# Layer 1's self-attention on quarters of TensorE's rows: the score products of four heads in two parts and a shift, with the maxima between them

## The chip, the cores and the metric

The kernel runs on one core of a Trainium2 chip. The metric is the device time in microseconds of one execution. Five engines work side by side and wait for each other through semaphores: TensorE (PE, with its weight loads listed as PEld), VectorE (DVE), ScalarE (ACT), GpSimd (POOL) and SyncE (SP), whose queue issues most of the transfers. Three runs of the kernel before took 2361.84, 2367.62 and 2370.89 us; the median is 2367.62.

## What is computed

The reference is a decoder of two layers on x (2 x 1024 tokens of 256). Each layer has self-attention, cross-attention and a feed-forward part, with a layer norm behind each. The change lies in the second layer's self-attention (layer 1), 16 heads of 16 dimensions:

```python
def _L1_attn_ref(x, W_qkv, b_qkv, W_proj, b_proj):
    NUM_HEADS, HEAD_DIM = 16, 16
    qkv = x @ W_qkv + b_qkv
    ...
    scores = jnp.einsum('bhqd,bhkd->bhqk', q, k) * HEAD_DIM ** -0.5
    attn = jax.nn.softmax(scores, axis=-1)
    out = jnp.einsum('bhqk,bhkd->bhqd', attn, v)
    ...
    return out @ W_proj + b_proj
```

The scores are 2 x 16 x 1024 x 1024, and the softmax runs over 1024 keys.

## The kernel before, in words

TensorE multiplies `lhsT` (the weights, loaded first) with `rhs` (streamed, up to 512 columns) into a bank of PSUM. The stacks here are in the format F32R. To keep precision, queries and keys are split by `l1_project` (L1167) into a high part and a rest: `qh`, `ql`, `kh`, `kl`. A product is then (qh + ql)(kh + kl), four partial products of 16 rows each.

`l1_attn` (L1197) handles four heads, a *quad*, at a time. The 16 **steps** (L1259) are batch x quad x half of the queries (512). A step has 8 **units**, one for each 128 keys (`kt`); there are 128 units. `stacks` (L1246) copies the parts by DMA into stacks for two heads each: 64 rows for a head, with the queries as qh, ql, qh, ql and the keys as kh, kh, kl, kl. A matmul of 64 rows so adds all four partial products at once, and two heads of a stack sit on the two halves of TensorE's rows. Each quad has two key and two query stacks: 4 x 8 = 32 transfers of 64 KB. SP's queue issues them, and ScalarE's half of those of the first quad (L1251).

The softmax needs the row maxima before the exponentials. `maxima` (L1262) computes scores with queries as rows: two matmuls (L1277) into two banks of the pool `bank` (three banks, L43 and L58), and VectorE takes the negated maximum of each bank (L1287). A step needs 16 such calls, two to a unit, nine units ahead of the products. `shifts` and `shifted` (L1291, L1303) turn a step's maxima into rows (four small VectorE operations, four transposes on TensorE at L1308, a copy at L70).

`products` (L1314) computes scores with keys as rows, two `wide` tiles (two banks each, two tiles in the pool) to a unit: for each, two matmuls of 64 rows (L1322) and two more (L1328) that add the shift through `pick`, a tile of ones and zeros. ScalarE takes the exponential of each wide tile (L1334). `mix` (L1341) multiplies the weights of the unit before with the values: four heads on four column tiles of 32 (L1348), an ordinary F32 matmul. After each step `taken` and `quotient` (L1355, L1359) copy the sum, transpose it (L1368) and divide.

The order is written out by hand (L1458 to L1488): nine early units of maxima into wide tiles (L1282), with projections and values between them; then for each unit, first call of maxima, products, second call of maxima, at a step's end the shift, then the mix of the unit before, then what `extra` holds for this unit (projections, stacks, values, normalisation). All three of TensorE, VectorE and ScalarE run in exactly this order. The stage begins at about 1690 us and its last mix is near 2160 us.

Of the kernel before, what the change touches and what calls it, by code (L numbers as in the profile page):

```python
# [33 lines left out]
class Decoder:  # L34
# [1162 lines left out]
    def l1_attn(self):  # L1197
        nc, t = self.nc, self.t
        w, parts = self.l1w, self.l1parts
        wo = self.weight(t["L1_attn_W_proj"].rearrange("(c p) o -> p c o", p=P), 2, D)  # L1200
        with ExitStack() as s:
            pool = lambda n, k: s.enter_context(self.pool(n, k))
            one, stp, qkp, rawp = pool("la1", 1), pool("st", 2), pool("qk", 1), pool("raw", 1)
            self.l1qkp = qkp

            pick = []
            for k in range(2):
                f = self.weight(None, 1, P)[:, 0, :]
                nc.gpsimd.memset(f, 0.0)
                for a in range(k, 4, 2):  # L1210
                    nc.gpsimd.memset(f[32 * a : 32 * a + 32, :], 1.0)
                pick.append(one.tile([P, P], F32R, name=f"pick{k}"))
                nc.vector.tensor_copy(pick[k], f)

            zeros = [one.tile([P, 4, 4, 32], F32, name=f"cz{k}") for k in range(2)]
            for cz in zeros:
# [2 lines left out]
            def project(b, m, name, blk):  # L1219
                self.l1_project(b, m, name, blk, self.xT[2 * b + blk])  # L1220
# [21 lines left out]
                    )  # L1242

            stack = {}

            def stacks(b, jp, name):  # L1246

                st = stack[b, jp, name] = stp.tile([P, S], F32R, tag=name, name=f"{name}st", bufs=4)
                for a in range(2):
                    at = 32 * (jp % 4) + 16 * a  # L1250
                    by = nc.scalar if a and b == 0 and jp < 2 else nc.sync  # L1251
                    for i, x in enumerate((0, 1, 0, 1) if name == "q" else (0, 0, 1, 1)):
                        by.dma_start(
                            st[64 * a + 16 * i : 64 * a + 16 * i + 16, :].bitcast(F32),
                            parts[name, b, jp // 4][x][at : at + 16, :],
                        )


            steps = [(b, quad, qb) for b in range(B) for quad in range(4) for qb in range(2)]  # L1259
            most, shift = {}, {}  # L1260

            def maxima(u, early=False):  # L1262

                if u >= 16 * len(steps):
                    return
                n, k = u // 16, u % 16 // 8
                qt, kb = divmod(u % 8, 2)
                b, quad, qb = steps[n]
                jp = 2 * quad + k
                if u % 16 == 0:  # L1270
# [4 lines left out]
                for a in range(2):  # L1275
                    rows = slice(64 * a, 64 * a + 64)
                    nc.tensor.matmul(  # L1277
                        sc[a], lhsT=stack[b, jp, "q"][rows, q0 : q0 + P],
                        rhs=stack[b, jp, "k"][rows, kb * 512 : (kb + 1) * 512], start=True, stop=True,
                    )  # L1280
                if early:
                    nc.vector.tensor_reduce(  # L1282
                        most[n][:, kb, qt, k : k + 3 : 2], both, AX.X, ALU.max, negate=True
                    )
                for a in range(0 if early else 2):
                    h = 2 * a + k
                    nc.vector.tensor_reduce(  # L1287
                        most[n][:, kb, qt, h : h + 1], sc[a], AX.X, ALU.max, negate=True
                    )

            def shifts(n):  # L1291

# [21 lines left out]
            def products(n, kt):  # L1314

                b, quad, qb = steps[n]
                ps = [self.wide(), self.wide()]
                for k in range(2):
                    q, keys = (stack[b, 2 * quad + k, name] for name in "qk")
                    for a in range(2):  # L1320
                        rows = slice(64 * a, 64 * a + 64)
                        nc.tensor.matmul(  # L1322
                            ps[k][:, a, :], lhsT=keys[rows, kt * P : (kt + 1) * P],
                            rhs=q[rows, qb * 512 : (qb + 1) * 512], start=True, stop=False,
                        )
                    for a in range(2):
                        rows = slice(64 * a, 64 * a + 64)
                        nc.tensor.matmul(  # L1328
                            ps[k][:, a, :], lhsT=pick[k][rows, :], rhs=shift[n][rows, :],
                            start=False, stop=True,  # L1330
                        )
                slot = self.weight(None, 2, S)
                for k in range(2):
                    nc.scalar.activation(  # L1334
                        slot[:, k, :], ps[k].rearrange("p a q -> p (a q)"), AF.Exp, scale=0.25
                    )
                return n, kt, slot.rearrange("p k (a q) -> p (k a) q", a=2)

            mixed = {}
# [86 lines left out]
            def at(unit, f, *args):  # L1426
                extra.setdefault(unit, []).append((f, args))
# [4 lines left out]
            last = 8 * len(steps)  # L1432
            both = [(name, blk) for name in "qk" for blk in range(2)]
            for n, (b, quad, qb) in enumerate(steps):
                first = 8 * n
                if qb == 0:
                    for i, (name, blk) in enumerate(both):
                        if quad % 2 == 0 and n > 4:
                            at(first - 26 + i, project, b, quad // 2, name, blk)
                    for i, name in enumerate("qk" if n else ()):  # L1440
                        for k in range(2):
                            at(first - 20 + 2 * k + i, stacks, b, 2 * quad + k, name)
                    if quad == 0 and n:
                        for k in range(4):
                            at(first - 22 + k, values, b, k)
                at(first + 8, taken, n)
                at(first + 9, quotient, n)
                if quad == 3 and n < len(steps) - 1:
                    g = 2 * b + qb
                    for k, f in ((10, turned), (11, output), (13, normed), (15, onward)):  # L1450
                        at(first + k, f, g)

            def others(unit):
                for f, args in extra.pop(unit, ()):
                    f(*args)

            engines = {mybir.EngineType.PE, mybir.EngineType.DVE, mybir.EngineType.Activation}
            with self.tc.manual_schedule(engines=engines):  # L1458
                for k in range(2):
                    for name in "kq":  # L1460
                        stacks(0, k, name)
                jobs = [lambda k=k: values(0, k) for k in range(4)]
                jobs += [lambda a=a: project(0, 1, *a) for a in both]
                for unit in range(-9, 0):
                    maxima(2 * unit + 18, True)
                    maxima(2 * unit + 19, True)
                    if jobs:
                        jobs.pop(0)()
                    others(unit)
                shifts(0)  # L1470
                shifted(0)
                late = None
                for unit in range(last + 1):

                    n = (unit + 1) // 8 if unit % 8 == 7 else None
                    if n:
                        shifts(n)
                    maxima(2 * unit + 18)
                    now = products(*divmod(unit, 8)) if unit < last else None
                    maxima(2 * unit + 19)  # L1480
                    if n:
                        shifted(n)
                    if late:
                        mix(*late)
                    late = now
                    others(unit)
                for unit in sorted(extra):
                    others(unit)  # L1488
# [607 lines left out]
```

## Time and profile before

| | |
|---|---|
| median of three runs | 2367.62 us |
| the profiled execution | 2366.31 us |
| its span, first to last instruction | 2364.4 us |
| mean granted TensorE clock | 0.982 |
| maxima on banks, VectorE (L1287) | 476 of 683 ns |
| matmuls for them (L1277) | 476 of 479 ns |
| products (L1322), shifts (L1328) | 512 each, median 393 ns for L1322 |
| exponentials, ScalarE (L1334) | 256 of 1022 ns |
| mix (L1348) | 1024 of 621 ns in the records |

The profile counts a matmul's time up to its result; the next one starts well before that, so distances between starts are read instead of durations. "Idle before, releaser" at the end of a group's line is the time that the engine stood before these instructions and what ended it. In the timeline, equal instructions that follow each other are merged (x2, x4), with the time of the first start and the time to the last end.

### The profile page before, as it was taken

How to read it: one execution, taken by the hardware profiler on the slowest of the kernel's cores; microseconds unless marked ns; L12 is line 12 of the kernel's file. 1: busy time of each engine (PE TensorE's matmuls, PEld its weight loads, DVE VectorE, ACT ScalarE, POOL GpSimd, SP SyncE). 2: the span in 40 equal slices, each digit the busy share in tenths (PEclk: the TensorE clock that was granted, in tenths of full speed). 3: DMA queues.
4: the chain of work that ended last, by engine and by line, in shares of the span. 5: the costliest groups of instructions: out<-in, count | busy, mean ns of one | idle time of the engine just before them, and what ended most of it. 6: DMA issues, size and time to landing. Idle time of an engine off the chain costs nothing.

```text
span 2364.4 us, 37096 instructions
## 1 busy us (share of the span) xinstructions
PE 2269.4 (96%) x13969; PEld 1568.0 (66%) x13969; DVE 1668.2 (71%) x2902; ACT 1107.6 (47%) x1730; POOL 907.5 (38%) x743
## 2 busy tenths in 40 slices
PE   8999999999998899999999999999999999999985
PEld 4555555555545678999999999999644444554752
DVE  5898888988786346545555555456789687995778
ACT  4666566566553323233233233333156455665346
POOL 4676576676565344413333333333200001002420
PEclk9999999999999999999999999999989999999988
DMA  6777677677685110101010001000303122210001
GB/s 153 175 180 171 150 181 170 146 179 174 140 200 126 41 61 1 36 10 35 19 31 26 29 31 36 15 1 1 70 12 50 19 37 36 41 32 1 1 1 36
DMA packets 103831, 168.67 MB, mean 71 GB/s; under 512 B 47603, under 2 KB 65509, under 8 KB 103653
## 3 DMA queue, kind: packets, MB, share of 16 engines
q1 hardware_dynamic: 96804, 147.94, 27.6%
q10 hardware_dynamic: 6848, 18.36, 3.1%
q8 instruction: 111, 1.82, 0.3%
q14 instruction: 68, 0.55, 0.1%
HBM read 34.10 MB, written 2.10 MB: 15 GB/s over the span
## 4 chain that ended last, share of the span: by engine, by line
PE 83%; DVE 9%; ACT 2%; issue 2%; SPq 2%; DMA 1%; POOL 1%; ACTq 0%; DVEq 0%; POOLq 0%
PE unit L1017 16%; PE acc L1065 10%; PE wide L325 9%; PE acc L410 8%; PE bank L1065 7%; PE acc L1348 5%; PE bank L280 4%; PE bank L1277 3%; DVE most L1287 3%; PE bank L428 2%; PE bank L740 2%; PE bank L304 2%; PE wide L1322 2%; PE wide L1328 2%; SPq L389 1%
## 5 line engine op out<-in xcount | busy, mean ns | idle before, releaser
L340 DVE TENSOR_REDUCE nm<-wide 128x1 f32<-128x1024 f32 x256 | 301.0, 1216 | 67.1 <-PE wide L325 66.0
L1334 ACT ACTIVATE w<-wide 128x1024 f32<-128x1024 f32 x256 | 248.2, 1022 | 142.9 <-PE wide L1328 133.5
L1287 DVE TENSOR_REDUCE most<-bank 128x1 f32<-128x512 f32 x476 | 295.7, 683 | 22.2 <-PE bank L1277 22.1
L325 PE MATMUL wide<-k,q 64*128 64x512 f32 x1024 | 262.4, 625 | 7.5 <-ACT p L345 6.7
L356 POOL TENSOR_SCALAR p<-p,sums 128x1024 f32<-128x1024 f32 x128 | 143.5, 1121 | 255.3 <-DVE sums L353 255.3
L410 PE MATMUL acc<-turned,v 128*64 128x256 f32 x2048 | 236.8, 384 | 3.3 <-DMA wq<-in_L_attn_w_q 3.3
L410 PEld LDWEIGHTS acc<-turned,v 128*64 128x64 f32 x2048 | 142.9, 137 | 115.7 <-issue 43.1
L1006 ACT ACTIVATE mhT<-mhT,cols 128x256 f32<-128x256 f32 (+1 forms) x256 | 143.4, 607 | 146.5 <-DVE mhT L1034 103.4
L345 ACT ACTIVATE p<-wide,nm 128x1024 f32<-128x1024 f32 x128 | 142.7, 1115 | 124.6 <-DVE nm L340 104.6
L915 POOL TENSOR_TENSOR hs<-hs,mhT 128x1024 f32<-128x1024 f32 x31 | 102.4, 3305 | 237.4 <-DVE hs L913 220.2
L1017 PE MATMUL unit<-xT,w 128*128 128x256 f32 x768 | 182.0, 379 | 0.0
L1074 DVE SCALAR_TENSOR_TENSOR r<-acc,gates,r 128x128 f32<-128x128 f32 x256 | 77.8, 345 | 138.1 <-PE acc L1065 138.1
L370 DVE STREAM_TRANSPOSE blocks<-p 128x1024 f32<-128x1024 f32 x128 | 158.1, 1235 | 20.5 <-DMA turned<-blocks 6.1
L325 PEld LDWEIGHTS wide<-k,q 64*128 64x128 f32 x1024 | 90.0, 188 | 121.4 <-issue 87.0
L370 DVE STREAM_TRANSPOSE blocks<-r 128x1024 f32<-128x1024 f32 x128 | 153.9, 1202 | 0.0
L1277 PEld LDWEIGHTS bank<-kst,qst 64*128 64x128 f32 x476 | 67.6, 188 | 127.8 <-DVE most L1287 105.9
L1017 PEld LDWEIGHTS unit<-xT,w 128*128 128x128 f32 x768 | 141.0, 190 | 17.1 <-issue 0.5
L1277 PE MATMUL bank<-kst,qst 64*128 64x512 f32 x476 | 138.5, 479 | 14.5 <-DVE most L1287 14.1
L356 POOL TENSOR_SCALAR r<-r,sums 128x1024 f32<-128x1024 f32 x128 | 143.6, 1122 | 0.0
L345 ACT ACTIVATE r<-wide,nm 128x1024 f32<-128x1024 f32 x128 | 142.2, 1111 | 0.2 <-POOL r L356 0.2
L180 POOL TENSOR_TENSOR rstd<-ve,nhalf 128x4 f32<-128x4 f32 (+3 forms) x17 | 14.2, 836 | 329.3 <-DVE ve L178 328.9
L1348 PE MATMUL acc<-w,v 128*32 128x512 f32 x1024 | 140.3, 621 | 0.0
(349 smaller groups left out, 4511.1 us busy)
## 6 DMA issues: line engine op xcount, KB each, us to landing
turned<-blocks SPq DMA_DIRECT2D x636, 128.0 KB, 2.4
turned<-blocks ACTq DMA_DIRECT2D x132, 128.0 KB, 2.5
w<-in_L_ffn_W SPq DMA_DIRECT2D x16, 1024.0 KB, 5.8
q<-q SPq DMA_DIRECT2D x64, 128.0 KB, 2.5
k<-k SPq DMA_DIRECT2D x32, 128.0 KB, 2.3
qst<-qh SPq DMA_DIRECT2D x48, 64.0 KB
qst<-ql SPq DMA_DIRECT2D x48, 64.0 KB, 2.3
kst<-kh SPq DMA_DIRECT2D x48, 64.0 KB, 2.3
```

The lines of the kernel that those rows point to most:

```text
L325: nc.tensor.matmul(sc[h][:, kb, :], lhsT=q[rows, qi, at : at + P], rhs=k[rows, ki, :], start=True, stop=True,)
L340: nc.vector.tensor_reduce(nm, sc, AX.XY, ALU.max, negate=True)
L345: nc.scalar.activation(p, sc.rearrange("p a c -> p (a c)"), AF.Exp, bias=nm, accum_out=sums[:, 0, h : h + 1],)
L356: nc.gpsimd.tensor_scalar(p, p, sums[:, 1, h : h + 1], 1.0, ALU.mult, ALU.mult)
L370: nc.vector.transpose(blocks[m][:, :, :, h, qt, :], p.rearrange("p (k r q) -> p r k q", r=4, q=32))
L410: nc.tensor.matmul(av[own[h], 0:256].rearrange("p (t i q) -> p i t q", t=2, i=4), lhsT=vals[u][:, kt, own[h]], rhs=p[:, h], start=kt == 0, ...
L1017: nc.tensor.matmul(v[:, m, :], lhsT=up[e][k][:, f : f + P], rhs=self.halves[g][k], start=k in (1, 2, 5) and m == 0, stop=True, skip_group_ ...
L1065: nc.tensor.matmul(ps[at][:, m * P : (m + 1) * P], lhsT=h[k][:, c, m * P : (m + 1) * P], rhs=down[e][k][:, c, :], start=k in (1, 2, 5) and ...
L1277: nc.tensor.matmul(sc[a], lhsT=stack[b, jp, "q"][rows, q0 : q0 + P], rhs=stack[b, jp, "k"][rows, kb * 512 : (kb + 1) * 512], start=True, s ...
L1287: nc.vector.tensor_reduce(most[n][:, kb, qt, h : h + 1], sc[a], AX.X, ALU.max, negate=True)
L1334: nc.scalar.activation(slot[:, k, :], ps[k].rearrange("p a q -> p (a q)"), AF.Exp, scale=0.25)
L1348: nc.tensor.matmul(mixed[n][o : o + 32, :], lhsT=vals[b][:, kt, 17 * h : 17 * h + 32], rhs=pT[:, a, :], start=kt == 0, stop=kt == 7, tile_ ...
```

## The change

Each head gets 32 rows, a quarter of TensorE's rows, instead of 64. The stacks hold four heads: queries as qh, ql (`qs`), and keys once as kh, kh (`kh`) and once as kl, kl (`kl`). A product is now two matmuls of 32 rows that add up in PSUM, part 0 with `kh` and part 1 with `kl`. There are three stacks for a quad, 24 transfers. `pick` is one tile of ones. `maxima` makes both query tiles' maxima of a pair of heads (lower 0, 1 or upper 2, 3) and returns its two parts as functions; `products` does so with three, the last of them with the shift and the exponential. `scored` interleaves them. A unit still has four maxima of 512 columns on VectorE and two exponentials.

```diff
+            f = self.weight(None, 1, P)[:, 0, :]
+            nc.gpsimd.memset(f, 1.0)
+            pick = one.tile([P, P], F32R, name="pick")
+            nc.vector.tensor_copy(pick, f)
...
+            made = {"qs": (0, 1), "kh": (0, 0), "kl": (1, 1)}
+            def stacks(b, quad, name):
+                st = stack[b, quad, name] = stp.tile([P, S], F32R, tag=name, name=name)
+                for j in range(4):
+                    at = 64 * (quad % 2) + 16 * j
+                    by = nc.scalar if j % 2 and b == quad == 0 else nc.sync
+                    for i, x in enumerate(made[name]):
                         by.dma_start(
+                            st[32 * j + 16 * i : 32 * j + 16 * i + 16, :].bitcast(F32),
+                            parts[name[0], b, quad // 2][x][at : at + 16, :],
                         )
...
+            rows = [slice(32 * j, 32 * j + 32) for j in range(4)]
+            def maxima(u, pair, early=False):
...
                 both = self.wide() if early else None
                 sc = [both[:, a, :] if early else self.bank() for a in range(2)]
+                def part(i):
+                    for a in range(2):
+                        r = rows[2 * pair + a]
+                        nc.tensor.matmul(
+                            sc[a], lhsT=stack[b, quad, "qs"][r, q0 : q0 + P],
+                            rhs=stack[b, quad, ("kh", "kl")[i]][r, kb * 512 : (kb + 1) * 512],
+                            start=i == 0, stop=i == 1,
+                        )
+                def reduce():
+                    out = most[n][:, kb, qt, 2 * pair : 2 * pair + 2]
+                    if early:
+                        nc.vector.tensor_reduce(out, both, AX.X, ALU.max, negate=True)
+                    for a in range(0 if early else 2):
+                        nc.vector.tensor_reduce(out[:, a : a + 1], sc[a], AX.X, ALU.max, negate=True)
+                return [lambda: part(0), lambda: (part(1), reduce())]
...
+            def products(n, kt, slot, pair):
                 b, quad, qb = steps[n]
+                ps = self.wide()
+                st = lambda name: stack[b, quad, name]
+                def part(i):
+                    for a in range(2):
+                        r = rows[2 * pair + a]
+                        if i < 2:
+                            lhsT = st(("kh", "kl")[i])[r, kt * P : (kt + 1) * P]
+                            rhs = st("qs")[r, qb * 512 : (qb + 1) * 512]
+                        else:
+                            lhsT, rhs = pick[r, :], shift[n][r, :]
+                        nc.tensor.matmul(ps[:, a, :], lhsT=lhsT, rhs=rhs, start=i == 0, stop=i == 2)
+                def exponential():
...
+                return [lambda: part(0), lambda: part(1), lambda: (part(2), exponential())]
+            def scored(unit):
...
+                up = maxima(unit + 9, 1)
+                low = products(n, kt, slot, 0)
+                for i in range(2):
+                    low[i]()
+                    if up:
+                        up[i]()
+                low[2]()
+                high = products(n, kt, slot, 1)
+                high[0]()
+                up = maxima(unit + 9, 0)
+                for i in range(2):
+                    high[1 + i]()
+                    if up:
+                        up[i]()
...
+                    for i, name in enumerate(made if n else ()):
+                        at(first - 20 + i, stacks, b, quad, name)
...
+                for name in ("kh", "qs", "kl"):
+                    stacks(0, 0, name)
...
                 for unit in range(-9, 0):
-                    maxima(2 * unit + 18, True)
-                    maxima(2 * unit + 19, True)
+                    wide = [maxima(unit + 9, pair, True) for pair in (1, 0)]
+                    for i in range(2):
+                        for part in wide:
+                            part[i]()
...
-                    maxima(2 * unit + 18)
-                    now = products(*divmod(unit, 8)) if unit < last else None
-                    maxima(2 * unit + 19)
+                    now = scored(unit)
```

More of the change, by code (lines that the diff above doesn't have):

```diff
@@ L1204, in l1_attn @@
             self.l1qkp = qkp
[L1206 to L1213, printed above, removed]
+            f = self.weight(None, 1, P)[:, 0, :]
+            nc.gpsimd.memset(f, 1.0)
+            pick = one.tile([P, P], F32R, name="pick")
+            nc.vector.tensor_copy(pick, f)
             zeros = [one.tile([P, 4, 4, 32], F32, name=f"cz{k}") for k in range(2)]
@@ L1244, in l1_attn @@
             stack = {}
[L1246 to L1252, printed above, removed]
+            made = {"qs": (0, 1), "kh": (0, 0), "kl": (1, 1)}
[5 more added lines that the diff above has]
+                    for i, x in enumerate(made[name]):
                         by.dma_start(
-                            st[64 * a + 16 * i : 64 * a + 16 * i + 16, :].bitcast(F32),
-                            parts[name, b, jp // 4][x][at : at + 16, :],
+                            st[32 * j + 16 * i : 32 * j + 16 * i + 16, :].bitcast(F32),
+                            parts[name[0], b, quad // 2][x][at : at + 16, :],
                         )
@@ L1260, in l1_attn @@
             most, shift = {}, {}
[L1262 to L1267, printed above, removed]
+            rows = [slice(32 * j, 32 * j + 32) for j in range(4)]
+            def maxima(u, pair, early=False):
+                if u >= 8 * len(steps):
+                    return []
+                n, (qt, kb) = u // 8, divmod(u % 8, 2)
                 b, quad, qb = steps[n]
-                jp = 2 * quad + k
-                if u % 16 == 0:
+                if u % 8 == 0 and pair:
                     most[n] = self.sm.tile([P, 2, 4, 4], F32, tag="most", name="most")
@@ L1274, in maxima @@
                 sc = [both[:, a, :] if early else self.bank() for a in range(2)]
[L1275 to L1289, printed above, removed]
+                def part(i):
[13 more added lines that the diff above has]
+                return [lambda: part(0), lambda: (part(1), reduce())]
             def shifts(n):
@@ L1312, in shifted @@
                 self.evac(shift[n], ps, by=nc.vector)
-            def products(n, kt):
+            def products(n, kt, slot, pair):
                 b, quad, qb = steps[n]
-                ps = [self.wide(), self.wide()]
-                for k in range(2):
-                    q, keys = (stack[b, 2 * quad + k, name] for name in "qk")
+                ps = self.wide()
+                st = lambda name: stack[b, quad, name]
+                def part(i):
                     for a in range(2):
[L1321 to L1331, printed above, removed]
-                slot = self.weight(None, 2, S)
[L1333 to L1336, printed above, removed]
@@ new lines, in part @@
+                        r = rows[2 * pair + a]
[6 more added lines that the diff above has]
+                def exponential():
+                    nc.scalar.activation(
+                        slot[:, pair, :], ps.rearrange("p a q -> p (a q)"), AF.Exp, scale=0.25
+                    )
@@ new lines, in products @@
+                return [lambda: part(0), lambda: part(1), lambda: (part(2), exponential())]
+            def scored(unit):
+                n, kt = divmod(unit, 8)
+                if unit >= last:
+                    return None
+                slot = self.weight(None, 2, S)
+                up = maxima(unit + 9, 1)
[12 more added lines that the diff above has]
+                        up[i]()
@@ L1439, in l1_attn @@
                             at(first - 26 + i, project, b, quad // 2, name, blk)
-                    for i, name in enumerate("qk" if n else ()):
-                        for k in range(2):
-                            at(first - 20 + 2 * k + i, stacks, b, 2 * quad + k, name)
+                    for i, name in enumerate(made if n else ()):
+                        at(first - 20 + i, stacks, b, quad, name)
                     if quad == 0 and n:
@@ L1458, in l1_attn @@
             with self.tc.manual_schedule(engines=engines):
-                for k in range(2):
-                    for name in "kq":
-                        stacks(0, k, name)
+                for name in ("kh", "qs", "kl"):
+                    stacks(0, 0, name)
                 jobs = [lambda k=k: values(0, k) for k in range(4)]
```

## The prediction

> **What bounds the kernel now.** I read the page's busy times first, then its costliest groups, then the waits of the stretch that the change touches (1720 to 2135 us), then one plain unit of it in the timeline. On the page TensorE has the largest share; that share is an average, so it says only where to look.
>
> ```profile
> PE 2269.4 (96%) x13969; PEld 1568.0 (66%) x13969; DVE 1668.2 (71%) x2902; ACT 1107.6 (47%) x1730; POOL 907.5 (38%) x743
> ...
> L1287 DVE TENSOR_REDUCE most<-bank 128x1 f32<-128x512 f32 x476 | 295.7, 683 | 22.2 <-PE bank L1277 22.1
> ...
> L1277 PE MATMUL bank<-kst,qst 64*128 64x512 f32 x476 | 138.5, 479 | 14.5 <-DVE most L1287 14.1
> ```
>
> The reader is to see 476 maxima of 683 ns: four to a unit, in 119 units. The waits between the two engines go both ways:
>
> ```profile
> PEld bank L1277 <- DVE most L1287: 105.9, 132, 2.6
> ...
> DVE most L1287 <- PE bank L1277: 22.1, 73, 1.7
> ```
>
> One plain unit, from the first matmul of its maxima (1903.42) to the next unit's (1906.12), 2.70 us:
>
> ```profile
> 1903.42 0.51 PE L1277 MATMUL bank<-kst,qst 64*128 64x512 f32 x2
> ...
> 1903.76 0.40 PE L1322 MATMUL wide<-qst,kst 64*128 64x512 f32 x2
> ...
> 1903.95 2.49 DVE L1287 TENSOR_REDUCE most<-bank 128x1 f32<-128x512 f32 x4 [0.21 <-PE bank L1277]
> 1903.99 0.39 PE L1328 MATMUL wide<-c,pick 64*128 64x512 f32 x2
> ...
> 1904.22 0.39 PE L1322 MATMUL wide<-qst,kst 64*128 64x512 f32 x2
> ...
> 1904.45 0.39 PE L1328 MATMUL wide<-c,pick 64*128 64x512 f32 x2
> 1904.46 0.42 PEld L1277 LDWEIGHTS bank<-kst,qst 64*128 64x128 f32 x2
> ...
> 1904.68 0.52 PE L1277 MATMUL bank<-kst,qst 64*128 64x512 f32 x2
> ...
> 1905.13 1.06 PE L1348 MATMUL acc<-w,v 128*32 128x512 f32 x8
> ```
>
> Each row with x2 is a pair on the two halves of the rows; pairs follow each other every 0.23 us (1903.76, .99, 1904.22, .45, .68), so I call 0.23 a round. The first maxima take 0.34 (to 1903.76), four rounds of products 0.92, the second maxima 0.45 to the mix at 1905.13, the mix 0.99. TensorE is the bound, since VectorE waits 0.21 for the unit's first bank and then does four maxima in 2.49. But VectorE is close, and it is held by banks: there are three, each maximum frees one, and the fourth bank of a unit is the first one again. Its weight load is inside the row 1904.46: it ends at 1904.88, so it began about 1904.70, just after the first maximum ended (1903.95 + 0.68 = 1904.63). Four rounds of products lie between the two pairs of maxima; they are what hides the first maximum.
>
> **The change, step by step.** A plain unit now has 12 matmuls on halves in six rounds. It gets 20 on quarters: 8 for maxima (two parts each), 12 for products (two parts and the shift). Written order: low part 0 with maxima of the upper pair part 0; low part 1 with upper part 1; low shift with high part 0; high part 1 with maxima of the lower pair part 0; high shift with their part 1. If four quarters run abreast, that is five rounds.
>
> *Round of four.* No row of before has four row tiles at once. Lower bound 0.23, the round of two; upper bound 0.46, two rounds of two. I take 0.23: the mix runs four column tiles abreast, eight weight loads of it within 0.16. The Trainium skill ("TensorE: Matmul & The Clock Gate", section "Measured speedup vs the span model") gives 3.07 times for four row tiles, so four tiles cost 1.30 of one; by it a round would be 0.30, the chain below would grow by 0.14 in each unit, and the sum by 17 us; no run here shows it yet.
>
> *The rounds saved count for nothing, because the new order moves the bank wait.* With t = 0 at the unit's first weight load: a first matmul really starts 0.11 later (weight loads of the next pair begin that long after). The upper pair's second part starts at 0.11 + 0.23 = 0.34. A result reaches VectorE 0.42 after its matmul's start (1903.95 - 1903.42 - 0.11), so the first maximum starts at 0.76 instead of 0.53 and ends at 1.44. The lower pair's second matmul needs the bank that this maximum reads: the third bank was free, the fourth is the first again. TensorE reaches it in round four, at 0.11 + 3 x 0.23 = 0.80, and issues in order, so it stands until 1.44 + 0.06 = 1.50. Queued behind it are the high shift, hence ScalarE's second exponential, the maxima's part 1, and the mix. After it: 0.34 to the part 1 (as at 1903.42 to 1903.76), 0.33 from there to the mix (the 0.45 above without its own load of 0.11, rounded), 0.99 for the mix: 1.50 + 0.34 + 0.33 + 0.99 = 3.16. Plain unit: **+0.46 us**. VectorE then has 0.67 idle in each, ScalarE (two of 1022 ns) ends at about 3.05, so neither binds.
>
> *Steps of eight units.* In a step without other work (first maxima at 2044.78 and 2068.37 in the timeline) 23.6 us are five or so units of 2.70, one of 3.85 with the shifts, and 3.29 and 2.90 after the quotient; in these three VectorE is late. With 0.67 of slack it no longer is: the four transposes cost TensorE 0.59 (2050.19 to 2050.78), so two units become 3.16 + 0.59 = 3.75 and six are 3.16, together 26.5: +2.9 for eight, +43 for 119 units.
>
> *Units with other work* (projections, values, normalisation, some 24). There VectorE or a chain PE, ACT, DVE, PE sets the pace; the longer wait is only the second round of the maxima, 0.23, or about 0.1 where VectorE is full. I take 0.2 less than the average 0.36 for each: -5.
>
> *The start.* Three stacks instead of four, 24 transfers instead of 32 per quad, each 0.6 us of issue on its queue. But the first maximum now needs all three, where it needed one pair of stacks. And the query stack takes the place in memory that the second key stack had, which waits for the last use of a tile of the layer before. The lines:
>
> ```profile
> 1688.32 0.39 PE L1065 MATMUL acc<-w2s,mhT 128*128 128x128 f32 x2
> ...
> 1690.42 0.73 PE L1277 MATMUL wide<-kst,qst 64*128 64x512 f32 x4
> ...
> 1691.20 2.41 SPq L1253 DMA_DIRECT2D kst<-xg  x4
> ...
> 1691.38 2.33 DVE L1282 TENSOR_REDUCE most<-wide 128x2 f32<-128x1024 f32 x2
> ```
>
> As the changed program is laid out, the query stack's first transfer waits for that acc matmul (it ends at 1688.7). Eight transfers on each of two queues follow: the last is issued at 1688.8 + 7 x 0.61 = 1693.1 and lands some 2.8 us later (2.3 to landing, 0.5 of issue), at 1695.9; the first maximum starts at about 1696.4 instead of 1691.38: +5. In the nine early units the lower pair's part 0 must wait for its wide tile before the upper pair's part 1 can go: +0.17 each, +1.5. TensorE idles 5 us more, which may bring half clock, as it stands at 0.91 over 1719 to 1800: between 0 and 3, taken as 1.5. Start: +8. Later stacks are ready in time: 24 x 0.63 + 2.8 = 18 us from the end of the units that release them, and seven units are over 22.
>
> *The last nine units* have no maxima: low and high overlap in one round only, five rounds instead of four, +0.23 x 9 = +2. The removed pick tile (one 0.28 cast, five small memsets) lies beside the wait at the start: 0.
>
> *Sum.* 43 - 5 + 8 + 2 = 48 us on the profiled execution's 2366.3 (span 2364.4 and 1.9 around it): **2414 us**. The median of the runs is 2367.6, 1.3 above that execution, within the runs' spread of 9.
>
> **Rivals.**
> 1. *The change does not do what it says: quarters run only two at once.* Rounds become 0.46. The first maximum then starts at 0.11 + 3 x 0.23 + 0.42 = 1.22, the fourth bank is free at 1.97, and the rest is 0.34 + 0.23 (one more pair) + 0.33 + 0.99, so 3.86: +1.16 in 119 units is 138 us, less the units with slack: about 2500. For it: only pairs are seen on rows. Against: the four column tiles of the mix. Partly so: 2440 to 2480.
> 2. *Not slower: the bank wait does not bind.* If TensorE reaches the fourth bank after 1.50 us anyway, or the first maximum ends before round four, nothing stands in its way: five rounds end the maxima at 1.25, the mix would end at 2.35, and VectorE's four maxima, 2.49, become the bound: -0.21 in five of eight units, 119 x 5/8 x 0.21 = -16, with +8 and +2 about 2360; were all units to gain and the start cost nothing, 2341. The point from which it decides is a first maximum ending by 0.80. For it: VectorE already fills 2.49 of 2.70. Against: the weight load at 1904.70, which already waits for that maximum, four rounds after the first pair instead of two.
>
> **How the numbers follow.** Forecast case 2390 to 2440, chance 0.72. Its low end has the weight load after the wait hidden and a result 0.05 sooner (-0.16 in 119 units, -19) and the start at +3; its high end has a round a third of the way from 0.23 to 0.46, 0.31 (+0.16 in 119 units, +19), and the clock's full 3, with some 5 for what is not seen. Partly abreast, 2440 to 2480: 0.08. Two at once, 2500: 0.07. No bank wait: 0.09, of which 0.05 below 2354 and 0.04 around 2360. Smaller still but slower, 2378 to 2390: 0.04. The range 2378 to 2460 holds 0.72 + 0.04 + 0.04 = 0.80. Half a per cent, about what a measurement of this kernel can tell from no change, is 12 us: faster 0.05, same 0.04, slower 0.91.
>
> **What would show it.** Right: plain units 3.1 to 3.3 us apart; four matmuls of 32 rows starting together; weight loads of the lower pair's maxima waiting some 0.7 us for the maxima of the same unit, and VectorE waiting about 0.6 us for TensorE in each unit where it waited 0.21; first maximum near 1696. Wrong: matmuls of a round starting in two groups 0.23 apart (rival 1); four maxima back to back with units of 2.5 (rival 2); or units above 3.16 for a wait on an exponential that I hold to be covered.

## The result and the profile after

The changed kernel took 2423.36 us (median of four runs, 2422.67 to 2426.97), the kernel before 2367.05 beside it (four runs). The ratio is 1.0242, with a 95% interval of 1.022 to 1.0265: **slower by 56 us**, eight more than the 48 of the forecast and inside its range.

The page of the changed kernel has nearly the same shares as before. TensorE has a thousand more matmuls, but only 20 us more of busy time. The line that moved is that of the maxima: VectorE stood 22 us ahead of them before, now 52. The matmuls that feed them stood 15 us for a maximum, now 47:

```profile
PE 2289.4 (95%) x14988; PEld 1552.0 (64%) x14993; DVE 1681.0 (69%) x2901; ACT 1119.5 (46%) x1730; POOL 904.0 (37%) x738
...
L1287 DVE TENSOR_REDUCE most<-bank 128x1 f32<-128x512 f32 x476 | 306.6, 686 | 51.9 <-PE bank L1276 46.9
...
L1276 PE MATMUL bank<-kh,qs 32*128 32x512 f32 x476 | 173.0, 488 | 47.2 <-DVE most L1287 45.3
```

The waits of the stage (1720 to 2195 us), with their total, their number and the longest:

```profile
PEld bank L1276 <- DVE most L1287: 96.7, 119, 2.8
...
PEld wide L1328 <- ACT w L1331: 73.7, 86, 1.7
DVE most L1287 <- PE bank L1276: 46.9, 77, 2.1
PE bank L1276 <- DVE most L1287: 45.3, 94, 2.4
```

The first line is smaller than before (105.9), and yet this is the wait that made the kernel slower. The length of such a wait is not what it costs. The matmuls' own wait (the last line: 14.1 with 14 waits before, 45.3 with 94 now) did grow, but in e1 below it is 16.6 with 15 waits in a kernel that is just as slow; the distances between starts tell. The second line is new and looks like a wait for an exponential; the experiments show that it is not one that counts.

One plain unit of the changed kernel in the timeline, from its first matmul (2077.26) to that of the next (2080.45):

```profile
2077.26 0.50 PE L1328 MATMUL wide<-qs,kh 32*128 32x512 f32 x2
...
2077.27 0.50 PE L1276 MATMUL bank<-kh,qs 32*128 32x512 f32 x2
...
2077.60 0.40 PE L1328 MATMUL wide<-qs,kl 32*128 32x512 f32 x2
2077.61 0.41 PE L1276 MATMUL bank<-kl,qs 32*128 32x512 f32 x2
...
2077.83 0.39 PE L1328 MATMUL wide<-c,pick 32*128 32x512 f32 x1
2077.84 0.39 PE L1328 MATMUL wide<-qs,kh 32*128 32x512 f32 x1
...
2078.05 2.63 DVE L1287 TENSOR_REDUCE most<-bank 128x1 f32<-128x512 f32 x4 [0.56 <-PE bank L1276]
2078.06 0.39 PE L1276 MATMUL bank<-kh,qs 32*128 32x512 f32 x1
...
2078.33 2.04 ACT L1331 ACTIVATE w<-wide 128x1024 f32<-128x1024 f32 x2 [1.14 <-PE wide L1328]
...
2078.79 0.18 PEld L1276 LDWEIGHTS bank<-kh,qs 32*128 32x128 f32 x1 [0.75 <-DVE most L1287]
2078.79 0.50 PE L1276 MATMUL bank<-kh,qs 32*128 32x512 f32 x1 [0.31 <-DVE most L1287]
...
2079.45 1.06 PE L1368 MATMUL acc<-w,v 128*32 128x512 f32 x8
2080.44 0.18 PEld L1328 LDWEIGHTS wide<-qs,kh 32*128 32x128 f32 x2 [0.84 <-ACT w L1331]
2080.45 0.50 PE L1328 MATMUL wide<-qs,kh 32*128 32x512 f32 x2
```

The reader is to see four quarters that start together (2077.26 and 2077.27), the third bank's matmul at 2078.06 alone, and its neighbour, the fourth, not until 2078.79: that bank is the one whose maximum began at 2078.05. The unit is 3.19 us long.

Where the 56 us are, by differences of the two traces. The first three rows go from the start of one mix to that of the next; the last three go from the first matmul of unit 0 to that of unit 119, and from there to the last mix:

| | before | after | difference | foreseen |
|---|---|---|---|---|
| plain unit | 2.70 | 3.18 | +0.48 | +0.46 |
| the two units with four transposes, in a step without other work | 3.86, 3.49 | 3.82, 3.77 | -0.04, +0.28 | to 3.75 each |
| step of eight without other work | 23.6 | 26.7 | +3.1 | +2.9 |
| 119 units with maxima | 416.0 | 461.9 | +45.9 | +38 |
| first matmul of unit 0 | 1719.2 | 1728.6 | +9.4 | +8 |
| last nine units | 26.7 | 27.6 | +0.9 | +2 |

### The profile page after: what moved, and what is told of

It reads as the page before. It is cut to its first block, busy times and chain, and to the rows that moved or that the text cites. A ratio compares the mean times of both kernels' runs of the same rounds, so it can differ in the third digit from the quotient of the medians.

```text
span 2420.5 us, 39092 instructions
## 1 busy us (share of the span) xinstructions
PE 2289.4 (95%) x14988; PEld 1552.0 (64%) x14993; DVE 1681.0 (69%) x2901; ACT 1119.5 (46%) x1730; POOL 904.0 (37%) x738
## 4 chain that ended last, share of the span: by engine, by line
PE 83%; DVE 10%; ACT 2%; issue 2%; DMA 1%; SPq 1%; POOL 1%; ACTq 0%; DVEq 0%; POOLq 0%
PE unit L1017 16%; PE acc L1065 9%; PE wide L325 9%; PE acc L410 9%; PE bank L1065 7%; PE acc L1368 5%; PE bank L280 4%; DVE most L1287 4%; PE bank L1276 4%; PE wide L1328 3%; PE bank L304 2%; PE bank L428 2%; PE bank L740 2%; PE bank L1186 1%; PE acc L1722 1%
## 5 line engine op out<-in xcount | busy, mean ns | idle before, releaser
L1287 DVE TENSOR_REDUCE most<-bank 128x1 f32<-128x512 f32 x476 | 306.6, 686 | 51.9 <-PE bank L1276 46.9
L1331 ACT ACTIVATE w<-wide 128x1024 f32<-128x1024 f32 x256 | 259.5, 1023 | 178.3 <-PE wide L1328 165.9
L1276 PE MATMUL bank<-kh,qs 32*128 32x512 f32 x476 | 173.0, 488 | 47.2 <-DVE most L1287 45.3
L1276 PE MATMUL bank<-kl,qs 32*128 32x512 f32 x476 | 137.4, 429 | 0.0
```

What stands on the lines that cost most here:

```text
L1276: nc.tensor.matmul(sc[a], lhsT=stack[b, quad, "qs"][r, q0 : q0 + P], rhs=stack[b, quad, ("kh", "kl")[i]][r, kb * 512 : (kb + 1) * 512], st ...
L1287: nc.vector.tensor_reduce(out[:, a : a + 1], sc[a], AX.X, ALU.max, negate=True)
L1331: nc.scalar.activation(slot[:, pair, :], ps.rearrange("p a q -> p (a q)"), AF.Exp, scale=0.25)
```

## The experiments

The layers ahead of this stage end up to 9 us earlier or later from one trace to the next (the group "acc<-w2s,mhT" of L1065, the last of the layer ahead, starts between 1686.05 and 1694.81). So beside the times I give the stretch from the start of that group to the end of the kernel, which leaves this out: 677.7 in the kernel before, 734.4 in the changed one.

**e1: is it the bank?** The theory is that of the prediction. Its rivals are the exponential that the waits name, and longer rounds. The lower pair's maxima are issued behind all high products; the products then no longer wait for the fourth bank, but the unit still does.

```diff
                 high[0]()
+                high[1]()
+                high[2]()
                 up = maxima(unit + 9, 0)
-                for i in range(2):
-                    high[1 + i]()
-                    if up:
-                        up[i]()
+                for f in up:
+                    f()
```

> The changed kernel with one move in each unit: the lower pair's maxima are issued after all of the high products, so that the high shift and ScalarE's second exponential no longer stand behind the wait for the fourth bank. Theory (the first maximum of the unit holds the fourth bank until 1.50 us after the unit's start): that moment does not move, and what follows it is the same 0.34 + 0.33 + 0.99, so plain units stay at 3.18 us and the time at 2423, within 5. Rival A (the unit is long because the second exponential starts late, and the next unit's products wait for it, as the page's releasers say: weight loads of L1328 after ScalarE): the exponential starts about 0.45 earlier, so units fall by up to 0.45, the time towards 2370. Rival B (the time goes into matmul rounds on quarters): seven rounds in a row instead of five, so +0.46 in a unit, some 2475.

Measured: 2426.07 us, ratio 1.0246 (1.021 to 1.0282), plain units 3.18, steps 26.6. The products are done earlier, and nothing is won. Its timeline:

```profile
2078.49 0.49 PE L1328 MATMUL wide<-qs,kh 32*128 32x512 f32 x2
...
2079.53 0.40 PE L1328 MATMUL wide<-c,pick 32*128 32x512 f32 x2
2079.56 1.94 ACT L1331 ACTIVATE w<-wide 128x1024 f32<-128x1024 f32 x2 [1.24 <-PE wide L1328]
2080.02 0.18 PEld L1276 LDWEIGHTS bank<-kh,qs 32*128 32x128 f32 x1 [0.53 <-DVE most L1287]
...
2081.67 0.18 PEld L1328 LDWEIGHTS wide<-qs,kh 32*128 32x128 f32 x2 [0.84 <-ACT w L1331]
```

The last shift is issued at 2079.53, 1.04 after the unit's first matmul and in its fifth round, so rounds are not longer. The second exponential begins right behind the first one and is over at 2079.56 + 1.94 = 2081.50, before the next unit (2081.67). The fourth bank still comes 1.53 after the unit's start (2078.49 to 2080.02), and the unit is as long as ever. So the rival of longer rounds falls. For the exponential this is a weak test: the second one stands behind the first in both kernels, so it moved only from 2.08 to 1.99 us after the unit's start (2079.35 in the unit above, 2080.48 here), not by the 0.45 that was expected. A trace of e8, below, settles it.

**e2 and e8: two doses of a shorter maximum.** If the bank ends the unit, whatever the first maximum loses, the unit loses too. The maxima run over the first 256 (e2) or 128 (e8) of their 512 columns.

```diff
-                        nc.vector.tensor_reduce(out[:, a : a + 1], sc[a], AX.X, ALU.max, negate=True)
+                        nc.vector.tensor_reduce(out[:, a : a + 1], sc[a][:, 0:256], AX.X, ALU.max, negate=True)
```

> The changed kernel with one cut: VectorE's maxima of the 119 units cover the first 256 of the 512 columns of each bank (half of the keys are left out of the maxima; all matmuls stay). By the rows for 512 (683 ns) and 1024 columns (1216 ns) such a maximum takes about 0.42. Theory: the fourth bank comes free 0.27 earlier, and VectorE has slack, so every plain unit falls from 3.18 to 2.91 and the time by 119 x 0.27 = 32 to about 2391 (2383 to 2399). Rivals A (exponentials) and B (matmul rounds): VectorE is not on the chain, no change, 2423 within 5.

> The changed kernel with each maximum over the first 128 of its 512 columns (the maxima leave out three quarters of the keys; the softmax divides the shift out again). A second dose after the 256 columns that gave units of 2.91 and 2389. Theory: with 256 columns the fourth bank still comes 0.4 after TensorE could use it, so another 0.135 of VectorE's work comes off each unit in full: plain units 2.78 (2.76 to 2.82), steps of eight near 23.4, 2389 - 119 x 0.135 = 2373 (2369 to 2378). Rival H (at 256 columns the wait is all gone, and something else ends the unit): units stay at 2.91, 2387 to 2391.

Measured: e2 2389.04 us, 1.009 (1.0057 to 1.0122), plain units 2.91; e8 2369.85, 0.9995 (0.9981 to 1.001), plain units 2.78. Both units are as expected to the hundredth: 0.27 and again 0.13 off each. The maxima have become much shorter, and in a unit of e2 VectorE stands for 1.39 us and works for 1.52:

```profile
2078.72 0.76 DVE L1287 TENSOR_REDUCE most<-bank 128x1 f32<-128x256 f32 x2 [1.09 <-PE bank L1276]
...
2079.20 0.18 PEld L1276 LDWEIGHTS bank<-kh,qs 32*128 32x128 f32 x1 [0.49 <-DVE most L1287]
...
2079.78 0.76 DVE L1287 TENSOR_REDUCE most<-bank 128x1 f32<-128x256 f32 x2 [0.30 <-PE bank L1276]
```

VectorE is nearly half idle and still sets the pace, by one instruction's end: 2079.20 is 0.48 behind 2078.72. Only with maxima over a quarter of the columns is the changed kernel level with the one before. A unit of e8 also shows that the next one does not wait for its second exponential:

```profile
2102.95 1.94 ACT L1331 ACTIVATE w<-wide 128x1024 f32<-128x1024 f32 x2 [0.84 <-PE wide L1328]
2103.02 0.18 PEld L1276 LDWEIGHTS bank<-kh,qs 32*128 32x128 f32 x1 [0.35 <-DVE most L1287]
...
2104.67 0.18 PEld L1328 LDWEIGHTS wide<-qs,kh 32*128 32x128 f32 x2 [0.84 <-ACT w L1331]
```

The two exponentials are over at 2102.95 + 1.94 = 2104.89, and the next unit had begun 0.22 before that. The rival of the exponential falls.

**e3 and e9: the same cut in the kernel before.** The prediction holds that four rounds of products hide the first maximum there. Then a shorter one should bring nothing to a unit.

```diff
-                        most[n][:, kb, qt, h : h + 1], sc[a], AX.X, ALU.max, negate=True
+                        most[n][:, kb, qt, h : h + 1], sc[a][:, 0:256], AX.X, ALU.max, negate=True
```

> The kernel before with the same cut (maxima over the first 256 of 512 columns, half of the keys left out of them). Theory: there the four rounds of products cover the first maximum, so plain units stay at 2.70 within 0.03; only the units where VectorE is late fall (3.85 to 3.29 and 2.90 to 2.70, 0.76 in a step of eight, 11 us in all, and a few in the units with other work): 2353 (2346 to 2359), less than half of what the same cut gives the changed kernel. Rival C (VectorE's maxima set the pace of every unit in both kernels): plain units fall here as there, by 0.27, and the time to 2335 or below.

Measured: 2338.24 us, 0.9875 (0.9843 to 0.9907); plain units 2.58 to 2.59, steps 21.9. Neither was right: the unit lost 0.12, not 0 and not 0.27. In its timeline the second pair's weight load follows the round ahead of it at once:

```profile
2027.82 0.40 PE L1322 MATMUL wide<-qst,kst 64*128 64x512 f32 x2
...
2028.52 0.40 PE L1328 MATMUL wide<-c,pick 64*128 64x512 f32 x2
2028.53 0.19 PEld L1277 LDWEIGHTS bank<-kst,qst 64*128 64x128 f32 x2
...
2028.76 0.39 PE L1277 MATMUL bank<-kst,qst 64*128 64x512 f32 x2
```

The next matmul starts a round after the one before it, 2028.52 to 2028.76: the load is hidden. Before the cut (in the rows of the prediction) that load began about 1904.70, when the round was all but over, and its own 0.11 lay bare: 0.45 from there to the mix instead of the 0.33 that the prediction used elsewhere. So the kernel before too paid for the fourth bank, 0.12 in each plain unit, and without that it is 2.58 long. A step without other work lost 1.7; its two units with transposes gained most (3.86 and 3.49 became 3.17 and 3.22). The second run of the same kernel stands with e7 below.

**e4: the place in memory at the start.** An unused tile of 8 KB a partition is put between the key and the query stack of the first quad, so that the query stack no longer lies where the layer ahead still works.

```diff
                     stacks(0, 0, name)
+                    if name == "kh":
+                        stp.tile([P, 2048], F32, tag="room", name="room", bufs=1)
```

> The changed kernel with an unused tile of 8 KB a partition between the key and the query stacks, so that none of the first three stacks lies where the layer before still reads its weights; nothing else differs. Theory (the start costs 7 us of waiting for the place, and the clock falls in the wait): transfers of the query stack start some 5 us earlier, the first maximum moves from 1698.4 to about 1691, and the time falls by 7 to 2416 (2412 to 2419). Rival D (the start is late because the first maximum needs 24 transfers instead of 16, whatever the place): the first maximum stays after 1696, and the time within 3 of 2423.

Measured: 2411.99 us, 1.0181 (1.0151 to 1.0212), the stretch 724.2, so 10.2 shorter than without the tile. The two starts, in the timeline of the changed kernel first:

```profile
1688.13 0.51 SPq L1250 DMA_DIRECT2D qs<-xg  x1
...
1693.73 1.61 PE L1276 MATMUL wide<-kh,qs 32*128 32x512 f32 x4 [3.85 <-DMA qs<-xT]
...
1697.33 1.31 PE L1276 MATMUL wide<-kl,qs 32*128 32x512 f32 x4 [1.99 <-DMA kl<-xg]
...
1698.42 2.36 DVE L1285 TENSOR_REDUCE most<-wide 128x2 f32<-128x1024 f32 x2 [7.76 <-PE wide L1276]
```

and of e4:

```profile
1683.79 0.53 SPq L1250 DMA_DIRECT2D qs<-xg  x1
...
1691.42 0.51 PE L1276 MATMUL wide<-kh,qs 32*128 32x512 f32 x4
...
1691.77 0.68 PE L1276 MATMUL wide<-kl,qs 32*128 32x512 f32 x4
1692.23 2.36 DVE L1285 TENSOR_REDUCE most<-wide 128x2 f32<-128x1024 f32 x2
```

In the changed kernel SP's first query transfer goes at 1688.13, 2.1 behind the start of the last acc group (1686.05), and TensorE stands for two DMAs. In e4 it goes at 1683.79, 3.9 ahead of that group (1687.66), no row here waits for a DMA, and the first maximum is 4.58 behind the group's start, as before (4.73), instead of 12.38. Three stacks in place of four, each of which the first maximum needs, cost nothing by themselves; the place did.

**e5 and e6: one part instead of two.** The maxima come from the keys' high part alone, one matmul each, and the upper pair's go first; e6 has the unused tile as well. The shift is then a little off the true maximum, and the softmax divides it out again.

```diff
-                            start=i == 0, stop=i == 1,
+                            start=True, stop=True,
...
-                return [lambda: part(0), lambda: (part(1), reduce())]
+                return [lambda: (part(0), reduce())]
...
+                high = products(n, kt, slot, 1)
+                low[0]()
+                for f in up:
+                    f()
+                low[1]()
+                high[0]()
+                low[2]()
+                high[1]()
+                high[2]()
+                for f in maxima(unit + 9, 0):
+                    f()
```

> The changed kernel with maxima from part 0 alone (queries times the high part of the keys; the softmax divides the shift out again, so the shift need not be the exact maximum, and the low part of the keys is left out of the maxima only), 16 matmuls in four rounds to a unit, the lower pair's maxima after the high products. Theory: the first maximum starts a round earlier, at 0.53, and the fourth bank is free at 0.53 + 0.68 + 0.06 = 1.27 instead of 1.50; after it 0.44 to the mix, without the second part, and 0.99: plain units 2.70, as in the kernel before, although TensorE has two rounds less than there and stands for 0.47 in each. Steps of eight go back to 23.6, which gives 46 us, and the start, which needs two stacks instead of three, some 5: 2372 (2366 to 2380). Rival B (matmul rounds): one round less than the changed kernel, 0.23 x 119 = 27 us, 2396. Rival E (VectorE's four maxima, 2.49, bind once TensorE has room): plain units 2.50, about 2355.

> Maxima from part 0 alone and the unused tile between the stacks, together. Theory: both gains add up, the start becomes that of the kernel before (first maximum near 1691), plain units 2.70: 2366 (2360 to 2372), the same as the kernel before within half a per cent. Rival E: about 2350. Rival B: 2389.

Measured: e5 2381.16 us, 1.0053 (1.0034 to 1.0073); e6 2375.46, 1.0028 (1.0016 to 1.0039). Plain units are 2.74 in both, steps 23.8: of the 0.48 that the change cost in a unit, 0.44 go with the second part, its round and the order that both parts need. Both times are 9 above what was expected; the stretch from the acc group is 680.3 in e6 (677.7 before), and the layers ahead of it, which the edit does not touch, end 6.6 and 6.9 us later in these two traces than in that of the kernel before. I have no cause for that. A unit of e6:

```profile
2037.53 0.50 PE L1328 MATMUL wide<-qs,kh 32*128 32x512 f32 x2
...
2038.10 2.48 DVE L1287 TENSOR_REDUCE most<-bank 128x1 f32<-128x512 f32 x4 [0.26 <-PE bank L1276]
...
2038.34 0.40 PE L1328 MATMUL wide<-c,pick 32*128 32x512 f32 x2
...
2038.85 0.18 PEld L1276 LDWEIGHTS bank<-kh,qs 32*128 32x128 f32 x1 [0.55 <-DVE most L1287]
```

The first maximum starts 0.57 behind the unit's first matmul instead of 0.79, and the fourth bank's load is 0.51 behind the last round (2038.34), where a round follows after 0.23: 0.28 of bank wait are left, with only four rounds to hide it.

**e7: one part, the tile, and maxima of 256 columns.** If those 0.28 are the bank, a maximum 0.27 shorter takes them away. It ran beside e9, the kernel before with the same cut.

> The changed kernel with the maxima from one part, the unused 8 KB tile, and each maximum taken over the first 256 of its 512 columns (the maxima leave out the keys' low part and half of the keys; the softmax divides the shift out again). Theory (the lower pair's fourth bank is what ends a unit): with one part and 512 columns a plain unit is 2.74, and the weight load of its last maximum stands 0.28 behind the end of the round ahead of it, for VectorE's first maximum. A maximum 0.27 shorter takes just that away: plain unit 2.47 (2.45 to 2.52), 119 units of 0.27 are 32, so 2375.5 - 32 = 2343 (2338 to 2350). Rival F (as in the kernel before with the same cut, where only 0.12 came off, since another wait or the weight load stood behind): units 2.62, 2361 (2356 to 2366). Rival G (TensorE's rounds hold the unit by now): units 2.70 to 2.74, 2371 to 2376.

> The kernel before with each maximum over the first 256 of its 512 columns (the maxima leave out half of the keys; the softmax divides the shift out again), beside quarters of rows with one part and the same cut on the same chip. As it gave 2338.2 with units of 2.585: 2338 to 2342. Theory: quarters with one part are then 0.1 per unit shorter, but their start and the units with other work give that back, so the two are within 6 us; rival F: quarters are slower by 20.

Measured: e7 2335.96 us, 0.9858 (0.9833 to 0.9883); e9 2337.91, 0.987 (0.9845 to 0.9894). e7 is 7 below what the theory gave. The first 119 units, from mix to mix, lost 38.0 (415.2 in e6, 377.1 here) and not 32, since the units with transposes (3.86 and 3.48 became 3.20 and 3.22) and those with other work gained more than the plain ones. Of the six plain units of a step four are 2.47 to 2.48, as the theory has it, and two are 2.60, held by something new:

```profile
2079.72 1.02 ACT L1331 ACTIVATE w<-wide 128x1024 f32<-128x1024 f32 x1
...
2080.07 0.49 PE L1328 MATMUL wide<-qs,kh 32*128 32x512 f32 x2
...
2080.79 0.18 PEld L1328 LDWEIGHTS wide<-qs,kh 32*128 32x128 f32 x2 [0.42 <-ACT w L1331]
...
2081.40 1.94 ACT L1331 ACTIVATE w<-wide 128x1024 f32<-128x1024 f32 x2 [0.67 <-PE wide L1328]
2081.68 0.16 PEld L1367 LDWEIGHTS acc<-w,v 128*32 128x32 f32 x8 [0.36 <-issue]
```

Here the high products wait for their wide tile, until the last exponential of the unit before has read it (2079.72 + 1.02 = 2080.74); this time the releaser named ended just ahead of the wait's end, and the wait counts. Steps are 21.5 against 21.9 of e9, and the stretch from the acc group 642.8 against 649.5. So quarters with maxima from one part save a little once the bank is out of the way, 6.7 us by the stretch; the two medians are 2 us apart, which is less than the two intervals can tell. Both are faster than the kernel before and the changed one, by 1.3% to 1.4% of the former. Nearly all of it comes from the shorter maxima, which leave out half of the keys (and in e7 the keys' low part as well), so that the shift no longer bounds the exponents of the other half: a price that the user of the kernel has to weigh.

## Why the prediction was right, and where it missed

**The round of four: right.** The rows of the unit above start at 2077.26, .60, .83 and 2078.06: 0.34 behind the first, as before, and then 0.23 apart, as two halves were. That settles rival 1 and "partly abreast". The Trainium skill ("TensorE: Matmul & The Clock Gate", section "Measured speedup vs the span model") gives 3.07 times for four row tiles, from which the prediction had estimated 0.30 by taking the round of two for the time of one tile; the trace does not agree with that estimate. The 3.07 itself, against one tile alone, is not measured here.

**The bank wait: right in every link of the sum.** The first maximum starts 0.79 after the unit's first load (0.76 foreseen), the fourth bank's load comes at 1.53 (1.50), the unit is 3.18 (3.16). e1 shows that it does not matter where in the unit the products stand, and e2 and e8 that a unit loses just what the first maximum loses. Rival 2 (the wait does not bind) asked for a first maximum ending by 0.80; it ended near 1.47. Of the signs against itself the prediction named a wait on an exponential. That wait is in the list of the profile (73.7 us, 86 times). But the low products at 2080.44 use the tile that the first of the two exponentials in the row 2078.33 reads, which is over near 2079.35; in e1 both are over 0.17 ahead of the next unit, and the unit is as long; in e8 the next unit begins 0.22 before they are over. What stands there is the 0.84 from the last weight load of the mix to the next unit's first, which e1, e2 and e7 show just alike, 0.99 from the mix's start; the kernel before had the same 0.99. The releaser named is only the last semaphore that came. One remark did not hold: the second exponential was to stand behind the wait for the bank, but it began when the first one was over (2078.33 and 2.04 for both), and cost nothing.

**The unit before: partly wrong.** "Four rounds of products are what hides the first maximum" was 0.12 short: e3 took that off each unit. The sum did not depend on it: its 2.70 was measured, and its 3.16 had left the bare 0.11 of the load out.

**The units with other work: the term of -5 was mis-sized; it came to about 0.** The 119 units took +45.9, against +43 - 5. The 2.9 of a step without other work was 3.1, which is 3 us in 119 units; 3.1 for every eight would be 46.1, so the units with other work took nothing off. The two normalisation units 12 and 13 do show a saving (from first matmul to first matmul, 4.85 and 4.97 became 4.86 and 4.84). The others carry +0.24, the second round that was foreseen, but more than the +0.16 on the average that -5 stands for (projections 5.30 to 5.54, values 4.87 to 5.11).

The largest piece goes with the clock. Units 18 to 20 do the same as units 10 to 12; before, they took 12.8 and 12.7 us. In the changed kernel units 10 to 12 took 4.86, 3.82 and 4.28, 13.0 in all, at a granted clock of 1.00. Units 18 to 20 took 5.35, 5.03 and 6.04, 16.4 in all, at 0.69: the records have half clock from 1804.5 to 1814.8. That is 3.5 us more. In e1, at 0.88, they took 13.8. Over all 119 units the half clock is 35 us against 28 before; another 10 us lie at the start (1691.9 to 1702.1). Why the clock fell just on units 18 to 20 is open. Two stretches at half clock, and the one with the plain unit:

```profile
1726.00:1740.00 14.00, 11.56 (x71) 5.70 (x72) 8.15 (x16) 5.81 (x6) 0.00 (x0) 0.51 0.00 0
1805.00:1815.00 10.00, 10.00 (x56) 4.16 (x54) 5.66 (x12) 3.65 (x4) 2.46 (x2) 0.51 0.01 2
2075.00:2083.00 8.00, 7.06 (x72) 2.76 (x69) 6.76 (x11) 5.57 (x6) 0.00 (x0) 1.00 0.01 2
```

The columns are the stretch, its length, busy times of the five engines, the granted clock (0.51, 0.51 and 1.00), the DMA share and the rate.

**The start: right in its cause, small in its size.** +9.4 instead of +8. The place in memory was worth 7.6 instead of 5, since the last of the three stacks landed at 1697.33 (1695.9 foreseen) and the first matmuls then ran at half clock (0.50 from 1692 to 1702; 758 to 791 ns each, against a mean of 488 in the stage). From the first maximum to unit 0 it is 2.4 more (30.2 against 27.8), where 3 had been put for the early units and the clock; and the layer ahead began its last group 0.6 earlier. e4 gave back 10.2 in all.

**The last nine units:** +0.9 instead of +2. The pick tile: 0, as foreseen; its cast stands at 1690.45 beside the wait for DMAs.

Sum: 48 foreseen, 56.2 found: 8 more in the units, 1 more at the start, 1 less at the end.

## What to carry to other kernels

Where two engines hand a ring of few buffers back and forth, a plan that saves one of them passes has first to be traced by buffer: when does the first one of the group come free, and when does the last of the group ask for it? Splitting a product into accumulated parts makes its buffer busy a round longer and its result a round later, and that can cost more than all the rounds it saves. The length of a wait in the list is not what it costs: the fourth bank's is 105.9 us for the weight loads and 14.1 for the matmuls before, 96.7 and 45.3 in the changed kernel, and 72.1 and 16.6 in e1, which is just as slow. A shorter version of the disputed instruction, in both kernels, tells.

## What was not expected of the hardware

- Four row tiles of 32 rows in F32R cost a round of 0.23 us, exactly as two of 64 rows do; no share of the fourth tile is paid.
- A weight load that began 0.24 us late (1904.70 instead of 1904.46) cost 0.12 us in each unit, though its matmul is hardly among the waits (14.1 us in all); e3 took both away.
- A maximum of 512, 256 and 128 columns from PSUM takes 686, 420 and 286 ns, and the second of two in a row adds 0.60, 0.34 and 0.21 us: a quarter of the columns still costs a third of the time of that second one.
- The stretch ahead of the stage, which no edit touched, ended within 1686.05 to 1694.81 us in eleven profiled executions; a difference under some 9 us is read from a stretch and not from the total.
